# Two attention layers on one core: the last v tile of a batch computed behind the first mixing instead of ahead of the second step's scores

## The chip, the cores and the metric

The kernel runs on one core of a Trainium2 chip. TensorE (PE in the profile) multiplies matrices into PSUM, ScalarE (ACT) and VectorE (DVE) read PSUM and write SBUF, GpSimd (POOL) does a few vector operations and issues some transfers, and SyncE (SP) issues most transfers. The metric is the device time of one execution in microseconds, as the median of several runs; smaller is better.

## The reference

The input is x of shape 8 x 512 x 32 x 32 in float32: eight batch elements (called batches here), 512 channels, 1024 positions. Two layers follow one another, each as x = x + layer(group_norm(x)).

Layer 0 is a plain attention block with 8 heads of 64 channels. Layer 1, in which the change lies, is attention whose scores are mixed between heads before the softmax:

```python
q = jnp.einsum('oc,bct->bot', w_q, xf).reshape(b, heads, hd, t)   # k, v likewise
attn = jnp.einsum('bhdq,bhdT->bhqT', q, k) * scale
attn = jnp.einsum('gh,bhqT->bgqT', w_head, attn)      # heads are mixed
attn = jax.nn.softmax(attn, axis=-1)
# the map of each head is then normalised by its mean and variance, with gamma and beta
out = jnp.einsum('bhqT,bhdT->bhqd', attn, v)
out = out @ w_proj.T + b_proj
```

All arithmetic is in float32.

## The kernel before

The first 1800 us are layer 0, batch by batch; the rest is layer 1, again batch by batch. All engines run their instructions in the order in which the program emits them (the whole is written under a manual schedule), so the order of calls in the source is the order of each queue.

**Layer 1, one batch.** Queries are cut into NT = 8 tiles of 128. A batch runs nine steps p = 0 to 8 of four quarters t = 0 to 3 (`Attention1.step`, L1847). Three kinds of work overlap, each one step behind the one before:

- `scores(p, i)`, L1621, i = 0 to 7: four matmuls into one two-bank PSUM buffer (L1628), then a copy to SBUF (`raw`), by ScalarE (L1640), and in step 0 for odd i by VectorE (L1638). Scores 0 to 3 fill one raw buffer, 4 to 7 a second one; there are two.
- `regroup(p, kh, s)`, L1642: when a raw buffer is full, SP issues two transfers for each of four slots, SBUF to SBUF, into the tile `re` (L1646), so that the heads of one query lie side by side. Sixteen transfers of 256 KB a step.
- `mix(p - 1, s)`, L1656, s = 0 to 3: matmuls with the head-mixing matrix, from `re` into two two-bank PSUM buffers (L1665), and two exponentials by ScalarE into a tile `e` (L1678).
- `flip(p - 1, s)` and `moments(p - 1, s)`, on VectorE: a transpose of `e` in 32 x 32 blocks into `et` (L1693), and four calls of batch statistics (L1704).
- `values(p - 2 or p - 1, u, ...)`: matmuls of v with `et` (L1720); they need the flips. Later `sums` (the `zz` rows, VectorE) and `totals` (z, L1757, TensorE) make the softmax sums.

In step 0 there are only scores. In step 1 scores of the second query tile come with the first mixings, and no values until its last quarter. From step 2 on all kinds overlap.

**v.** The v projection of a batch is eight tiles of 128 positions x 512 channels, each four matmuls of 128 x 128 weights (a tile of y) against 512 columns of the v weights. Each float32 matmul appears twice in the profile, so a tile is eight TensorE rows. `v_pair(b, i)` (L1446) computes two tiles into one two-bank PSUM buffer, then copies the first to SBUF on ScalarE (L1458) and the second on VectorE (L1459). Pairs 0 and 1 are made at the end of the batch before (for batch 0 by L1030), pairs 2 and 3 in step 0 of the batch's own attention.

**The place.** Work that belongs to no step is put into an `Agenda` under a slot number. `step` runs slot 4p + t at the end of each quarter, and some half slots inside a quarter: slot 4p - 0.5 in quarter 0, directly after `mix(p - 1, 0)` and ahead of `flip(p - 1, 0)`. Pair 2 stands in slot 1, pair 3 in slot 3, the end of step 0. In batch 0 `v_sums` (L1463, 128 small matmuls at L1471) follows in slot 3.

**Buffers.** `m_psum` (L1283) hands out three two-bank PSUM buffers in turn, to scores, mixings, v pairs and projections; a buffer is free again when its last reader is done. The y of a batch and its v are single buffers of the pool `shared` (L654): the load of the next batch's y, of which `piece` emits one quarter a step from step 1 on (L1337, on SP), waits until the last reader of the present y is done. The v weights lie in one of two buffers that `et` uses too.

Of the kernel before, what the change touches and what calls it, by code (L numbers as in the profile page):

```python
# [467 lines left out]
def tile_two_attention_layers(  # L468
# [19 lines left out]
    nc = tc.nc  # L488
# [175 lines left out]
    def group_stages(b0, b1, psum):  # L664

        gs = GroupStats(
            gstat, psum, mvs[:, b0:b1].rearrange("p b c s -> p (b c) s"), f"1_{b0}", keep=1
        )

        def end():  # L670
            gs.root()
            at = slice(b0 * NCC, b1 * NCC)
            nc.vector.tensor_copy(gmean[:, at], gs.gm)
            nc.vector.tensor_copy(grstd[:, at], gs.r1)
            nc.vector.scalar_tensor_tensor(
                gneg[:, at], gs.gm, -1.0, gs.r1, ALU.mult, ALU.mult
            )
            nc.vector.scalar_tensor_tensor(
                ys[:, b0:b1].rearrange("p b c -> p (b c)"), gs.dm, float(T), gs.r1,
                ALU.mult, ALU.mult,  # L680
            )

        return gs.means, gs.squares, end
# [13 lines left out]
    with ExitStack() as l0:  # L697
# [87 lines left out]
        n_t, xa_t, q_t, k_t, v_t = {}, {}, {}, {}, {}  # L785
# [89 lines left out]
        def combine_right(nm, n):  # L875

            if not tmp:
                for i in range(7):
                    tmp[i] = epool.tile([P, 2, FB], F32, tag="e", name=f"tmp_{nm}_{i}")
            b11, b12, b21, b22 = (n[:, 2 * i : 2 * i + 2, ts(j, FB)] for i in (0, 1) for j in (0, 1))  # L880
            nc.vector.tensor_sub(tmp[0], b12, b11)
            nc.vector.tensor_sub(tmp[1], b22, tmp[0])
            nc.vector.tensor_sub(tmp[2], b22, b12)
            nc.vector.tensor_sub(tmp[3], b21, tmp[1])
# [318 lines left out]
        for b in range(B):  # L1203
            more = b + 1 < B
            ag = Agenda()
# [61 lines left out]
    with ExitStack() as l1:  # L1267
# [15 lines left out]
        def m_psum(nm):  # L1283
            return ps_m.tile([P, 2, FB], F32, tag="m", name=nm)
# [4 lines left out]
        y_t, qo_t, k_t, v_t = ({0: t["1"]} for t in (n_t, q_t, k_t, v_t))  # L1289
# [12 lines left out]
        def left_piece(key, f, n):  # L1302

            if f == 0:
                left_tile(key)
            nc.sync.dma_start(
                out=w_t[key][:, f : f + n].rearrange("p f o -> p (f o)"),
                in_=left_d[key[0] + "1"][:, 2 * f * HC : 2 * (f + n) * HC],
            )
# [16 lines left out]
        def p_piece(c):  # L1326

            if c == 0:
                left_tile(("p", B - 1))
                w_t["p", B - 1] = w_t["p", B - 1][:, :NCC]  # L1330
            nc.sync.dma_start(out=w_t["p", B - 1][:, c], in_=w_projT[ts(c, P)])

        def y_piece(b, c):

            if c == 0:
                y_t[b] = shared.tile([P, NCC, T], F32, tag="n", name=f"y_{b}")
            nc.sync.dma_start(out=y_t[b][:, c], in_=x1_d[b][ts(c, P), :])  # L1337

        def normalize1(b, c):
            normalize_to(y_t[b][:, c], b, c)  # L1340
# [74 lines left out]
        def right_tile(b):  # L1415

            right_t[b] = rawpool.tile([P, 4, 2, FB], F32, tag="raw", name=f"right_{b}")

        def left_p(b):

            t = rawpool.tile([P, H * FB], F32, tag="raw", name=f"left_p_{b}")
            load_left(("p", b), t[:, : 14 * HC])

        def right_y(b, parts=range(4)):
            combine_right(right_t[b], y_t[b], parts)

        def k_projection(b):
            t = k_t[b] = shared.tile([P, NCC, T], F32, tag="k", name=f"k1_{b}")

            def finish(i, j, x, y):  # L1430
                dst = t[:, 2 * i : 2 * i + 2, ts(j, FB)]
                if y is None:
                    nc.scalar.copy(dst, x)
                else:
                    nc.vector.tensor_add(dst, x, y)

            return Projection(f"pk1_{b}", ("k", b), y_t[b], right_t[b], finish)
# [3 lines left out]
        def k_leave():  # L1441
            for fn in due:
                fn()
            due.clear()

        def v_pair(b, i):  # L1446

            if i == 0:
                v_t[b] = shared.tile([P, NT, C], F32, tag="v", name=f"v1_{b}")
            ps = m_psum(f"pv1_{b}_{i}")  # L1450
            w = w_t["v", b]
            for m in range(2):
                for c in range(NCC):
                    nc.tensor.matmul(  # L1454
                        ps[:, m], y_t[b][:, c, ts(2 * i + m, P)], w[:, c],
                        start=(c == 0), stop=(c == NCC - 1),
                    )
            nc.scalar.copy(v_t[b][:, 2 * i], ps[:, 0])  # L1458
            nc.vector.tensor_copy(v_t[b][:, 2 * i + 1], ps[:, 1])  # L1459

        vs = const_tile("vs", [P, H, B])

# [34 lines left out]
        def out_view(b):  # L1497


            return qo_t[b].rearrange("p (n two) a t -> p n (two a t)", two=2)  # L1500
# [413 lines left out]
        def load_wv(b):  # L1914

            t = etpool.tile([P, 8 * H * 64], F32, tag="et", name=f"wv_{b}")[:, : NCC * C]
            load_w(("v", b), wvT, t)
# [3 lines left out]
        NV = NT // 4  # L1921
        for b in range(B):
            more = b + 1 < B
            a = Attention1(b)
            ag = Agenda()
            for i in range(NV):
                ag.at(1 + 2 * i, lambda i=i: v_pair(b, NV + i))
            if b == 0:
                stages = group_stages(B - 1, B, small_psum1)
                for i in range(3):  # L1930
                    ag.at(i, stages[i])
                ag.at(3, v_sums)
            if more:
                a.pieces += [lambda c=c: y_piece(b + 1, c) for c in range(NCC)]
                a.pieces += [lambda f=f: left_piece(("k", b + 1), f, 2) for f in (0, 4)]
                ag.at(4 * NT, lambda: left_piece(("k", b + 1), 2, 2))
                ag.at(4 * NT, lambda: left_piece(("k", b + 1), 6, 1))
                for c in range(NCC):
                    ag.at(20 + c, lambda c=c: normalize1(b + 1, c))

                def k_go(*ms):
                    if not kp:
                        kp.append(k_projection(b + 1))
                    for m in ms:
                        kp[0].products(m)
                        due.append(lambda m=m: kp[0].leave(m))

                kp = []
                ag.at(4 * NT - 0.5, lambda: right_tile(b + 1))
                ag.at(4 * NT - 0.5, lambda: k_go(1))  # L1950
                ag.at(4 * NT, lambda: right_y(b + 1, [0, 1]))
                ag.at(4 * NT + 0.5, lambda: k_go(2))
                ag.at(4 * NT + 1, lambda: right_y(b + 1, [2, 3]))
                ag.at(4 * NT + 1, lambda: left_p(b))
                ag.at(4 * NT + 1.5, lambda: k_go(6))
                ag.at(4 * NT + 2.5, lambda: k_go(7))
            else:
                a.pieces += [lambda c=c: p_piece(c) for c in range(NCC)]
            for p in range(NT + 1):
                for t in range(4):  # L1960
                    a.step(p, t, ag)
            ag.flush()
            k_leave()
            last = NT - 1
            a.sums(last)
            if not more:
                a.values(last, 0, 2, 3)
                a.leave(last, 0)
                a.values(last, 1, 0, 1, 2, 3)
                a.leave(last, 1)  # L1970
                a.totals(last)
                a.instance()
                out1_last(a)
                continue
            k_go(5)
            a.values(last, 0, 2, 3)
            a.leave(last, 0)
            load_wv(b + 1)
            a.values(last, 1, 0, 1, 2, 3)
            a.leave(last, 1)  # L1980
            a.totals(last)
            a.instance()
            k_leave()
            k_go(4, 3)
            k_leave()
            a.instance_end()
            v_pair(b + 1, 0)
            a.divide(NCH - 1)
            for g in range(H):
                a.affine(g)  # L1990
            right_o = re_t[:, 4:8]
            combine_right(right_o, out_view(b))
            op = out1(b, right_o)
            load_left(("q", b + 1))
            v_pair(b + 1, 1)
            a.check()
            op.run()
            q_projection(b + 1).run()
# [70 lines left out]
```

## Time and profile before

| what | value |
|---|---|
| median of 3 runs | 3999.17 us (3997.65 to 4006.88) |
| the profiled execution's own time | 3999.31 us |
| its span, first to last instruction | 3997.5 us |
| layer 1 within it | from about 1800 us to the end |
| TensorE busy | 3885.5 us (97%) |
| VectorE busy | 2834.6 us (71%) |
| ScalarE busy | 1971.3 us (49%) |
| mean granted TensorE clock | 0.995 |
| v tile rows L1454 | 480, in 30 calls of `v_pair` (16 rows each) |
| last v pair of batch 3 | 2653.20 to 2660.33 us |
| batch 3's first score of step 1, first mixing, first flip, first z | 2660.26, 2663.00, 2666.68, 2686.12 us |

Rows of the timeline give start, length, engine, line, operation, output <- inputs, shapes, the number of merged rows, and in brackets how long the engine had been idle and who released it. A merged TensorE row can hold short waits inside itself, so its length can exceed its work. The list of waits gives the total, the number of times and the longest. In a chain of waits each line is what released the next one. A DMA row of a queue is the issue of the transfer; when it lands is read from the updates of its semaphore in the trace.

### The profile page before, as it was taken

Reading aid. Unit: us, or ns where it says so; the run is one execution under the profiler, and the core shown is the slowest. Engines: PE = TensorE matmul, PEld = TensorE weight load, DVE = VectorE, ACT = ScalarE, POOL = GpSimd, SP = SyncE. Lnnn points to the kernel's source line nnn. Section 1 sums busy time; section 2 is a strip of 40 time slices with the busy share of each in tenths; the row PEclk is TensorE's granted clock in tenths of the full one; section 3 lists DMA queues with packets and bytes.
Section 4 is the critical chain, followed back from the end, with each engine's and each line's share of the span. In section 5 each row is a group of like instructions: output and inputs, shape, how many; then the busy total and the mean of one; then the engine's idle time right before and its main releaser. Section 6 shows DMA issues by size and latency. Waiting matters only on the chain.

```text
span 3997.5 us, 95841 instructions
## 1 busy us (share of the span) xinstructions
PE 3885.5 (97%) x41932; PEld 1826.1 (46%) x41932; DVE 2834.6 (71%) x4124; ACT 1971.3 (49%) x2431; POOL 128.5 (3%) x150
## 2 busy tenths in 40 slices
PE   8999999999999999999999999999999999999997
PEld 4353535344343535344544535545545445445354
DVE  4748475766657584857958949859769679588597
ACT  1726363544536271615717528437257166175274
POOL 0000000000000000000100000000001000000010
PEclk9999999999999999999999999999999999999999
DMA  3313131111121111217828749658469288397384
GB/s 121 120 48 117 46 120 48 62 59 66 53 83 54 72 68 61 75 66 184 230 92 226 190 120 237 173 137 227 148 164 228 99 210 207 97 232 198 107 219 127
DMA packets 245883, 519.10 MB, mean 130 GB/s; under 512 B 47312, under 2 KB 54480, under 8 KB 238800
## 3 DMA queue, kind: packets, MB, share of 16 engines
q1 hardware_dynamic: 238912, 497.95, 43.2%
q0 software_dynamic: 6544, 14.94, 1.7%
q8 instruction: 331, 5.42, 0.6%
q14 instruction: 96, 0.79, 0.1%
HBM read 197.16 MB, written 46.92 MB: 61 GB/s over the span
## 4 chain that ended last, share of the span: by engine, by line
PE 81%; DVE 13%; ACT 2%; DMA 2%; issue 2%; SPq 0%; DVEq 0%
PE s L1084 11%; PE a L1110 11%; PE a L1720 7%; PE s L1628 7%; DVE bn L1704 6%; PE pk_p L902 6%; PE pq_p L902 5%; PE pv L1454 5%; PE pv_p L902 5%; DVE et L1693 5%; PE pp_p L902 5%; PE pk L1379 4%; PE pq L1379 4%; PE pp L1379 4%; PE m L1665 4%
## 5 line engine op out<-in xcount | busy, mean ns | idle before, releaser
L1693 DVE STREAM_TRANSPOSE et<-e 128x2048 f32<-128x2048 f32 x256 | 587.3, 2294 | 88.7 <-ACT e L1678 86.8
L1720 PEld LDWEIGHTS a<-et,v 128*64 128x64 f32 x16384 | 509.2, 138 | 296.2 <-issue 247.6
L1704 DVE BATCH_NORM_STATS2 bn<-e 128x6 f32<-128x512 f32 x1024 | 634.3, 675 | 0.0
L1089 ACT ACTIVATE e<-s 128x1024 f32<-128x1024 f32 x512 | 497.2, 1026 | 234.5 <-PE s L1084 232.1
L1640 ACT COPY raw<-s 128x1024 f32<-128x1024 f32 x480 | 470.2, 1018 | 226.1 <-PE s L1628 197.5
L1720 PE MATMUL a<-et,v 128*64 128x64 f32 x16384 | 557.0, 225 | 12.1 <-DVE et L1693 11.4
L1678 ACT ACTIVATE e<-m 128x1024 f32<-128x1024 f32 x512 | 496.2, 1021 | 126.5 <-PE m L1665 54.2
L1097 DVE TENSOR_TENSOR zacc<-zacc,e 128x1024 f32<-128x1024 f32 x384 | 468.7, 1221 | 87.2 <-ACT e L1089 64.9
L1628 PE MATMUL s<-k,q 64*64 64x512 f32 x4096 | 516.0, 608 | 6.2 <-DVE q L1493 3.1
L1084 PE MATMUL s<-q,k 64*64 64x512 f32 x4096 | 490.1, 593 | 2.3 <-ACT e L1089 2.3
L1110 PE MATMUL a<-e,v 64*64 64x512 f32 x4096 | 484.1, 589 | 0.0
L1665 PE MATMUL m<-re,wmix 32*32 32x512 f32 x8192 | 315.3, 604 | 19.3 <-DMA re<-raw 17.8
L1110 PEld LDWEIGHTS a<-e,v 64*64 64x64 f32 x4096 | 156.7, 133 | 282.8 <-issue 282.2
L1084 PEld LDWEIGHTS s<-q,k 64*64 64x64 f32 x4096 | 147.9, 133 | 275.2 <-issue 240.7
L1628 PEld LDWEIGHTS s<-k,q 64*64 64x64 f32 x4096 | 127.7, 132 | 220.8 <-issue 78.2
L1454 PE MATMUL pv<-wv,y 128*128 128x512 f32 x480 | 212.1, 597 | 0.0
L1736 ACT COPY q<-a 64x256 f32<-64x256 f32 x256 | 93.7, 366 | 184.7 <-PE a L1720 182.7
L1772 POOL DMA_DIRECT2D zd<-rz x56 | 34.7, 619 | 3449.0 <-DVE r L1784 3449.0
L1454 PEld LDWEIGHTS pv<-wv,y 128*128 128x128 f32 x480 | 89.3, 190 | 116.9 <-issue 110.3
L1665 PEld LDWEIGHTS m<-re,wmix 32*32 32x32 f32 x8192 | 66.7, 103 | 148.9 <-ACT raw L1640 58.6
L1458 ACT COPY v<-pv 128x512 f32<-128x512 f32 x30 | 17.6, 585 | 218.7 <-PE pv L1454 218.7
L1095 DVE TENSOR_TENSOR zacc<-e,e 128x1024 f32<-128x1024 f32 x64 | 78.3, 1223 | 56.1 <-ACT e L1089 56.1
(315 smaller groups left out, 3942.4 us busy)
## 6 DMA issues: line engine op xcount, KB each, us to landing
re<-raw SPq DMA_DIRECT2D x1024, 256.0 KB
left_q<-left_q SPq DMA_DIRECT2D x17, 1792.0 KB
left_p<-left_p SPq DMA_DIRECT2D x17, 1792.0 KB
left_k<-left_k SPq DMA_DIRECT2D x10, 1792.0 KB
x<-in_x_dram SPq DMA_DIRECT2D x32, 512.0 KB
rzb<-zd SPq DMA_DIRECT2D x128, 128.0 KB
x<-x SPq DMA_DIRECT2D x64, 256.0 KB
y<-x SPq DMA_DIRECT2D x32, 512.0 KB
```

The lines of the kernel that those rows point to most:

```text
L902: nc.tensor.matmul(out, st, mv, start=start, stop=(k == 1), skip_group_check=True)
L1084: nc.tensor.matmul(ps[c * D : c * D + D, m], k[r, hp, k0 : k0 + D], q[r, hp, ts(f, FB)], start=True, stop=True,)
L1089: nc.scalar.activation(e[i], ps, AF.Exp, scale=S0 * S0)
L1110: nc.tensor.matmul(acc[g][a][m * D : m * D + D], v[rows, kc, ts(2 * hp + m, D)], e[i][rows, m], start=(kc == 0), stop=(kc == NG - 1),)
L1379: nc.tensor.matmul(self.ps[m][:, i], w[:, left, k * HC + i * P : k * HC + i * P + P], right[:, k], start=(k == 0 and m != 2), stop=(k == 1 ...
L1454: nc.tensor.matmul(ps[:, m], y_t[b][:, c, ts(2 * i + m, P)], w[:, c], start=(c == 0), stop=(c == NCC - 1),)
L1628: nc.tensor.matmul(ps[c * D : c * D + D, m], qo_t[b][r, p, hp, ts(c, D)], k_t[b][r, hp, ts(kh, FB)], start=True, stop=True,)
L1665: nc.tensor.matmul(ps[a // 2][c * 32 : c * 32 + 32, a % 2].rearrange("p (r h k) -> p h r k", r=2, h=2), wmix[rows].rearrange("p g i -> p ( ...
L1678: nc.scalar.activation(e[:, :, 2 * h : 2 * h + 2].rearrange("p r a k -> p a r k"), ps[h].rearrange("p a (r k) -> p a r k", r=2), AF.Exp,)
L1693: nc.vector.transpose(self.et[p, u].rearrange("p kb (r st a) g q -> p st kb r (a g q)", r=2, st=2)[:, st], self.e[p, s].rearrange("p r a ( ...
L1704: nc.vector.bn_stats(self.bn[p][:, s, a], e[:, :, a].rearrange("p r k -> p k r"))
L1720: nc.tensor.matmul(acc[two * D : two * D + D, s].rearrange("p (x q) -> p x q", q=4), v_t[b][:, kb, ts(g, D)], et[:, kb, :, g], start=(kb = ...
```

## The change

`v_pair` takes a list of tiles, `ms`, of the pair to compute; called without it, it does both as before. Each call requests its own PSUM buffer. Pair 3 of every batch is split. Its first tile (with its ScalarE copy) stays in slot 3, at the end of step 0. Its second tile (with its VectorE copy) goes to slot 3.5, which `step` runs in quarter 0 of step 1: behind scores 0, 1, 2 and the first mixing, ahead of the first flip. Pair 2 stays in slot 1. In batch 0 `v_sums` now lies between the two tiles.

```diff
-        def v_pair(b, i):
+        def v_pair(b, i, ms=range(2)):
 
             if i == 0:
                 v_t[b] = shared.tile([P, NT, C], F32, tag="v", name=f"v1_{b}")
-            ps = m_psum(f"pv1_{b}_{i}")
+            ps = m_psum(f"pv1_{b}_{i}_{ms[0]}")
             w = w_t["v", b]
-            for m in range(2):
+            for m in ms:
                 for c in range(NCC):
                     nc.tensor.matmul(
                         ps[:, m], y_t[b][:, c, ts(2 * i + m, P)], w[:, c],
                         start=(c == 0), stop=(c == NCC - 1),
                     )
-            nc.scalar.copy(v_t[b][:, 2 * i], ps[:, 0])
-            nc.vector.tensor_copy(v_t[b][:, 2 * i + 1], ps[:, 1])
+            for m in ms:
+                copy = nc.vector.tensor_copy if m else nc.scalar.copy
+                copy(v_t[b][:, 2 * i + m], ps[:, m])
...
-            for i in range(NV):
-                ag.at(1 + 2 * i, lambda i=i: v_pair(b, NV + i))
+            ag.at(1, lambda: v_pair(b, NV))
+            ag.at(3, lambda: v_pair(b, NV + 1, [0]))
+            ag.at(3.5, lambda: v_pair(b, NV + 1, [1]))
```

## The prediction

> **What bounds the kernel now.** I read the page first, then the waits of TensorE, then the chain of waits around the place that changes, then the rows of the engines there. I use batch 3 of layer 1 throughout; batches 1, 2 and 4 to 7 have the same row lengths there within 0.02 us, and batch 0 differs by one extra block (L1471). The page, part 1:
>
> ```profile
> PE 3885.5 (97%) x41932; PEld 1826.1 (46%) x41932; DVE 2834.6 (71%) x4124; ACT 1971.3 (49%) x2431; POOL 128.5 (3%) x150
> ```
>
> 97% suggests no slack on TensorE, yet moving work pays only where TensorE really stands. The list of TensorE's waits:
>
> ```profile
> PE z L1757 <- DVE zz L1750: 29.1, 27, 2.1
> PE m L1665 <- DMA re<-raw: 17.8, 11, 3.3
> PE a L1720 <- DVE et L1693: 11.4, 10, 5.3
> PE m L1665 <- ACT e L1678: 1.4, 8, 0.2
> ```
>
> The z and a waits are for VectorE. Their first ones in each batch lie just behind the place that changes. The chain of waits in batch 3 (start, length, what):
>
> ```profile
> 2653.27 7.06 PE pv L1454 x16
> 2660.33 2.74 PE s L1628 x24
> 2663.07 1.61 PE m L1665 x29
> 2664.68 0.02 issue
> 2664.71 1.95 ACT e L1678 x2
> 2666.65 0.02 issue
> 2666.68 2.31 DVE et L1693
> 2668.99 1.01 DVE bn L1704 x2
> ...
> 2685.76 0.23 DVE zz L1750
> 2685.98 0.14 issue
> 2686.12 0.39 PE z L1757 x4
> ```
>
> So the path is: v pair, three scores and the first mixing on TensorE; the exponentials on ScalarE; then VectorE without a pause from 2666.68 to 2685.98 (four flips and moments, then zz); then TensorE again at z. While VectorE carries the path, TensorE stalls, as its timeline shows (start, length, instruction, idle before):
>
> ```profile
> 2663.00 1.58 PE L1665 MATMUL m<-re,wmix 32*32 32x512 f32 x32
> 2664.51 1.09 PE L1628 MATMUL s<-k,q 64*64 64x512 f32 x8
> 2665.78 2.05 PE L1665 MATMUL m<-re,wmix 32*32 32x512 f32 x32 [0.18 <-ACT e L1678]
> 2670.05 1.94 PE L1665 MATMUL m<-re,wmix 32*32 32x512 f32 x32
> 2673.64 1.15 PE L1720 MATMUL a<-et,v 128*64 128x64 f32 x32 [0.63 <-DVE et L1693]
> 2675.75 1.16 PE L1665 MATMUL m<-re,wmix 32*32 32x512 f32 x32
> ```
>
> A mixing takes 1.16 us when nothing holds it (2675.75) and 1.58, 2.05 and 1.94 in the first three quarters, where it waits in mid-group for PSUM to be emptied. From 2660.26 to 2673.64, 13.38 us, TensorE has six scores (0.91 each, from 2.74 for three) and three mixings (about 1.08 net of overlap): 5.5 + 3.2 = 8.7 us of work, so 4.7 us of hole, more than one v tile.
>
> [...] 97%, and a third of those 13.38 us is hole. [...] The three two-bank buffers here do rotate, and the 2.05 us mixing is that rotation running out. [...] every engine's rows follow the order in the code. This decides the prediction: the moved tile's copy stands in VectorE's queue ahead of the first flip. [...] Here a regrouping transfer's row is 0.53 us, and its semaphores finish 3.2 us after its start (2654.63 to 2657.83).
>
> **The change, part by part.** Times below are us after the first score of the second step (2660.26 before), called tau.
>
> *Removed at the end of step one.* Four fp32 matmuls, recorded as eight. A v pair of sixteen takes 7.06 us from its first row to the next group's; a second pair directly behind one costs 6.87 (14.00 - 7.13, the 32-record blocks). Half of 6.87 is 3.43 us. Its eight weight loads (0.19 us each) overlap and cost nothing apart. The first score of step two then starts 3.43 us earlier, if nothing else holds it. Its PSUM buffer was emptied earlier (the copies of scores 6 and 7 end by 2654.6), and the regrouping transfers that free its raw buffer landed by 2655.3. The other tile's ScalarE copy (0.58 us) stays where it is and is over before the first raw copy, as before. VectorE's copy (0.69 us) leaves; VectorE idles there (6.43 us before it), so that is worth 0.
>
> *Does the first mixing find its data?* It needs the tenth regrouping transfer of step one, at 2658.95 by the DMA semaphores. The mixing starts at 2663.00 now and would at 2659.57: the margin falls from 4.05 us (4.04 to 4.08 in batches 1 to 7, 7.88 in batch 0) to 0.62, of which about 0.14 is the wake-up seen where this wait does bind (the last mixing row of steps, e.g. 2812.45 to 2812.59). Hidden, by 0.5 us. The transfers themselves do not move: they are issued after the copy of score 7, ahead of the tile.
>
> *Added: the tile behind the first mixing.* Its PSUM buffer is the one of the third score, emptied at tau 4.05; the mixing ends at 4.25. So it starts at 4.2 and TensorE is free at about 7.9 (3.43 + 0.2 for the change of group, as 7.07 against 6.84 = 16 x 0.4275 shows). A pair's first copy starts 7.17 us after its first matmul; eight records less, 3.74. So VectorE's copy runs from about 7.97 to 8.6. The first flip, ready at 6.42 as before (exponentials don't depend on the tile), stands behind it and starts at about 8.6. That is the wait that the change adds: **2.2 us on the VectorE chain** (bounds 2.1 and 2.3: next row 0.61 or 0.69 us after the copy's start). Behind the flip stand all moments, flips and zz of this step, and behind these TensorE's a and z.
>
> *Everything else in the hole.* The fourth score (7.9), its raw copy (9.0 to 10.0), the second mixing (8.8; its second buffer is the tile's, empty at 8.6) and its exponentials (10.1 to 12.1) are late by 2 us too, but the second flip needs them only at 8.6 + 4.62 = 13.2. Third exponentials end at 16.3; third flip at 17.8. Values wait for the second flip until 15.5, as they do now until 13.38. From there all engines stand to one another as now. Cost 0; without VectorE's chain as cover these scores would cost the tile's full 3.4 us.
>
> *Queues.* SP: the load of the next batch's y (512 KB, L1337) writes the single y buffer that the tile still reads, so its issue moves from 2661.25 to the tile's end, about 2664.8. Behind it on SP stand step two's regroupings, due when score 3's raw copy ends (now 2667.57, then about 2666.9): 1.5 us to spare after its 0.6 us issue. Those regroupings come 0.6 us later against the flips than now. The next mixing that needs the group's tenth transfer has 0.53 to 1.43 us of margin, and TensorE's 1.23 us wait at z follows, so up to about that much is absorbed: 0. POOL issues nothing here. The weights wv keep their et buffer longer, until the third flip asks for it at 17.8: 0. The extra PSUM request shifts the rotation by one: 0.
>
> *Sum.* Per batch -3.43 + 2.2 = -1.23 us; eight batches have one such place (in batch 0 with v_sums between, and 3.4 us at half clock): **-9.8 us**. The profiled execution took 3999.31 us (span 3997.5, so 1.8 around it), which gives 3989.5; the median of the runs, 3999.17, lies 0.14 from it, so the forecast is 3989.4 either way: 0.25% less.
>
> **Rivals.**
> *Whole gain* (VectorE's delay is swallowed, or the copy comes before the exponentials end): 8 x 3.43 = 27.4 us, 3971.8. For: VectorE is only 71% busy. Against: it has no pause at all from the first flip to z, and TensorE waits there in every batch. Part of it, 12 to 20 us, if the copy comes earlier than worked out or a wait later in the batch shortens.
> *Nothing gained*: the tile delays the chain by its full length, e.g. because the mixing's release or the y load's place pushes the regroupings by more than z absorbs: 3999.2.
> *Slower*: the first mixing comes to wait for the regrouping. It decides from a tenth landing 0.5 us later than now; the gain is used up at 0.5 + 1.23 = 1.7 us later, and 0.3% is lost from 3.3 us later. For: later in each batch the same kind of wait does bind, 1.2 to 3.3 us. Against: at this place seven batches agree within 0.04 us, and the transfers' start does not move. At 3.5 us later: +1.8 x 8 = 14 us, 4013.
>
> **How the numbers follow.** A measurement of this kernel can tell about 0.3% (12 us) from no change. The forecast's own case 0.58 (3986.5 to 3991.5; one time in twelve or so a measurement of it crosses 12 us), more than 12 us gained 0.22, nothing gained 0.11, slower 0.09. Hence faster 0.27, same 0.64, slower 0.09. The range 3978 to 4000 holds the first case, the nearer half of the second and nearly all of the third.
>
> **What would show it.** Right: in each batch eight pv records ahead of the scores and eight behind the first mixing; the time from first score to that mixing still 2.74; a VectorE v copy directly ahead of the first flip, and that flip 2.2 us later after the first score (8.6 against 6.42); values at 15.5 against 13.38; z still waiting about 1.2 us; TensorE's mixings 1.1 to 1.2 rather than 2 us. Wrong: a wait for re<-raw at the first mixing, a first flip that starts at the exponentials' end, or a z wait that vanishes.

## The result, and the profile after

Over 22 runs of each kernel, taken turn by turn, the changed kernel has a median of 3996.7 us (3986.82 to 4004.14) and the kernel before 4001.79 us (3994.13 to 4010.3). The ratio is 0.9983, with a 95% interval of 0.9976 to 0.9989: 6.8 us or 0.17% faster (4.4 to 9.6 us). Two later sets of runs of the same changed kernel gave 0.9979 (0.9968 to 0.9990) and 0.9983 (0.9975 to 0.9992). That lies inside the predicted range and on the side that was forecast; the size forecast, 0.25% (9.8 us), was too large by 3 us. The prediction took 0.3% as the least that a measurement can tell from no change; with 22 runs of each kernel the interval is 0.13% wide and excludes no change. The profiled execution took 3989.87 us with a span of 3988.1, which is 9.4 us less than the first span before.

In the profiles below the lines of the code behind `v_pair` have moved by one: L1665 of before is L1666, and so on. The list of TensorE's waits after the change (total, times, longest):

```profile
PE z L1758 <- DVE zz L1751: 27.8, 26, 2.1
PE m L1666 <- DMA re<-raw: 20.5, 13, 3.4
PE a L1721 <- DVE et L1694: 6.9, 9, 4.5
```

The wait of the values for the flip (a, for et) has fallen by 4.5 us, and the wait of the mixing for the exponentials (m, for e) is gone from the list. The wait for the regrouping has grown from 17.8 to 20.5 us (18.4 and 19.7 in a second trace of each kernel). The chain of waits at the same place of batch 3:

```profile
2660.28 2.74 PE s L1629 x24
2663.01 1.51 PE m L1666 x29
2664.53 3.65 PE pv L1454 x8
2668.17 0.02 issue
2668.20 0.69 DVE v L1460
2668.89 2.22 DVE et L1694
...
2688.22 0.39 PE z L1758 x4
```

Before, the path went from the mixing over the exponentials to the first flip. Now it goes from the mixing through the moved tile and its VectorE copy to the first flip; the exponentials are ready 2 us earlier and wait. TensorE's timeline:

```profile
2662.94 1.58 PE L1666 MATMUL m<-re,wmix 32*32 32x512 f32 x32
2664.46 3.70 PE L1454 MATMUL pv<-wv,y 128*128 128x512 f32 x8
2669.11 1.16 PE L1666 MATMUL m<-re,wmix 32*32 32x512 f32 x32
2672.50 1.94 PE L1666 MATMUL m<-re,wmix 32*32 32x512 f32 x32
2675.76 1.15 PE L1721 MATMUL a<-et,v 128*64 128x64 f32 x32 [0.30 <-DVE et L1694]
```

The second mixing takes 1.16 us where it took 2.05: its buffers are free by the time it starts. The third still takes 1.94.

The table gives the starts of the first mixing, the first flip, the first values and z, in us after the first score of step 1. Batch 0, with its extra block (L1471), is left out.

| | first mixing | first flip | values | z |
|---|---|---|---|---|
| before, batches 1 to 7 | 2.74 | 6.41 | 13.38 | 25.85 |
| predicted | 2.74 | 8.6 | 15.5 | 28.0 |
| after, batches 1 and 3 to 7 | 2.74 | 8.59 | 15.55 | 28.02 |
| after, batch 2 | 3.87 | 9.30 | 16.27 | 28.72 |

### The profile page after: what moved, and what is told of

The parts are those of the page before. It is cut to its first block, busy times and chain, and to the rows that moved or that the text cites. A ratio compares the mean times of both kernels' runs of the same rounds, so it can differ in the third digit from the quotient of the medians.

```text
span 3988.1 us, 95834 instructions
## 1 busy us (share of the span) xinstructions
PE 3881.3 (97%) x41932; PEld 1825.2 (46%) x41932; DVE 2832.9 (71%) x4124; ACT 1974.8 (50%) x2431; POOL 128.7 (3%) x150
## 4 chain that ended last, share of the span: by engine, by line
PE 81%; DVE 13%; issue 2%; DMA 2%; ACT 2%; SPq 0%; DVEq 0%
PE s L1084 11%; PE a L1110 11%; PE a L1721 7%; PE s L1629 7%; DVE bn L1705 6%; PE pk_p L902 6%; PE pq_p L902 5%; PE pv L1454 5%; DVE et L1694 5%; PE pv_p L902 5%; PE pp_p L902 5%; PE pk L1379 4%; PE pq L1379 4%; PE pp L1379 4%; PE m L1666 4%
## 5 line engine op out<-in xcount | busy, mean ns | idle before, releaser
L1694 DVE STREAM_TRANSPOSE et<-e 128x2048 f32<-128x2048 f32 x256 | 587.6, 2295 | 47.7 <-ACT e L1679 44.7
L1666 PE MATMUL m<-re,wmix 32*32 32x512 f32 x8192 | 308.8, 608 | 21.1 <-DMA re<-raw 20.5
L1460 DVE COPY v<-pv 128x512 f32<-128x512 f32 x30 | 20.7, 690 | 160.4 <-PE pv L1454 81.7
L1666 PEld LDWEIGHTS m<-re,wmix 32*32 32x32 f32 x8192 | 65.5, 103 | 142.4 <-ACT raw L1641 59.8
```

Source lines behind the costliest of these rows:

```text
L1666: nc.tensor.matmul(ps[a // 2][c * 32 : c * 32 + 32, a % 2].rearrange("p (r h k) -> p h r k", r=2, h=2), wmix[rows].rearrange("p g i -> p ( ...
L1694: nc.vector.transpose(self.et[p, u].rearrange("p kb (r st a) g q -> p st kb r (a g q)", r=2, st=2)[:, st], self.e[p, s].rearrange("p r a ( ...
```

## The experiments

My theory was that of the prediction: removing the tile ahead of the scores wins 3.43 us a batch, and its copy, standing ahead of the first flip in VectorE's queue, gives 2.2 us of it back, one to one. The rivals were that VectorE does not set the end and only TensorE's hole counts, that the first mixing comes to wait for the regrouping, and, for the part of the gain that was missing, the granted clock. Every kernel was timed beside the kernel before.

**The copy on ScalarE.** Only the engine of the moved tile's copy changes.

```diff
             for m in ms:
-                copy = nc.vector.tensor_copy if m else nc.scalar.copy
+                copy = nc.vector.tensor_copy if m and len(ms) > 1 else nc.scalar.copy
```

> The changed kernel, but the moved v tile is copied out of PSUM by ScalarE, so that nothing stands ahead of the first flip in VectorE's queue. Theory of the prediction (the copy ahead of the flip costs the VectorE chain 2.2 us a batch): the first flip starts at 6.4 us after the first score of the second step again (8.6 in the changed kernel); the chain is then held only at its second flip, which waits for the exponentials of the second mixing at about 12.1 (11.0 before), so values and z are 1.1 us later than before and not 2.2; gain 3.43 - 1.1 = 2.3 us a batch, 17 to 19 us against before (about 0.45%). Rival (the VectorE chain isn't what sets the end, the gain is the idle time of TensorE that is filled): the same time as the changed kernel, 7 to 10 us below before.

Measured: 3984.37 us, ratio 0.9947 (0.9932 to 0.9962), 21 us below before (15 to 27). VectorE's rows in batch 3, whose first score is at 2658.28:

```profile
2664.69 2.31 DVE L1694 STREAM_TRANSPOSE et<-e 128x2048 f32<-128x2048 f32 x1 [8.68 <-ACT e L1679]
2666.92 2.48 DVE L1705 BATCH_NORM_STATS2 bn<-e 128x6 f32<-128x512 f32 x4
2670.44 2.31 DVE L1694 STREAM_TRANSPOSE et<-e 128x2048 f32<-128x2048 f32 x1 [1.04 <-ACT e L1679]
```

The first flip starts at 6.41 again, at the end of the exponentials, and the second one waits 1.04 us for its own. z stands at 27.00, 1.15 us later than before, as expected:

```profile
2685.27 0.39 PE L1758 MATMUL z<-sel,zz 128*64 128x32 f32 x4
```

Moving one copy of 0.6 us to another queue about tripled the gain. This is what the theory says and the rival excludes: TensorE's work and order are those of the changed kernel. Two things did not follow the expectation. The values come at 15.18, 1.8 us later than before and not 1.1, because now TensorE itself reaches them late (it does not wait there); its wait at z, 1.2 us before, shrinks to 0.6 us or less and hides this. And z is only 1.0 us earlier than in the changed kernel, which is 8 us in eight batches, of the 14 measured between the two. The mean clock of these five runs, 0.9944 against 0.9937 in the first 22 runs of the changed kernel, accounts for some 3 us more at the rate found below; the rest is within the interval.

**A delay on VectorE alone.** In the kernel before, the first flip of each batch is done twice; no other work moves (dst and src stand for the two views of L1694 and L1695).

```diff
-                nc.vector.transpose(dst, src)
+                for _ in range(2 if (p, s) == (0, 0) else 1):
+                    nc.vector.transpose(dst, src)
```

> The kernel before, with the first flip of each batch done twice on VectorE (same output). It measures by itself what a VectorE delay at this place is worth. Theory: it passes one to one: values and z 2.2 us later in every batch, 17 to 19 us slower than before (0.45%). Rival (VectorE, 71% busy, has slack that swallows it): 0.

Measured: 4023.12 us, ratio 1.0050 (1.0035 to 1.0064), 20 us slower (14 to 26). Values stand at 15.72 (+2.34) and z at 28.3 (+2.5) in batches 1 to 7. So a delay here passes to the end. But TensorE's rows show more than a delay:

```profile
2687.97 1.15 PE L1721 MATMUL a<-et,v 128*64 128x64 f32 x32 [2.98 <-DVE et L1694]
2689.06 1.81 PE L1628 MATMUL s<-k,q 64*64 64x512 f32 x8
2690.80 2.01 PE L1665 MATMUL m<-re,wmix 32*32 32x512 f32 x32
```

Behind the stall of 2.98 us a score takes 1.81 us and a mixing 2.01, where they take 1.09 and 1.16: the granted clock is at half for 3.4 us. The 1.23 us that TensorE otherwise waits at z hid most of that.

**Half of that delay.** Ahead of the first flip, half of it is done once more.

```diff
+                if (p, s) == (0, 0):
+                    nc.vector.transpose(dst[:, 0:4], src[:, 0:4])
                 nc.vector.transpose(dst, src)
```

> The kernel before, with half of the first flip of each batch done once more ahead of it on VectorE (same output): half the delay of double_flip, 1.15 us. In all traces so far a TensorE stall of 2 us or more is mostly followed by 3.4 us at half clock, one of under 1.5 us hardly ever; the stall at the values, 0.63 us before, grows to 2.9 in double_flip and to 1.8 here. Theory (VectorE delay passes one to one, the half clock comes on top and only behind long stalls): 8 to 11 us slower than before, z 1.2 us later, mean clock within 0.001 of before. Rival (the half clock follows the delay whatever its length): 15 us or more slower, mean clock 0.992 or less.

Measured: 4014.18 us, ratio 1.0030 (1.0020 to 1.0040), 12 us slower (8 to 16); z at 27.13 in five of the eight batches, +1.27. The delay passes one to one (1.27 x 8 = 10 us). The mean clock of the timed runs was 0.9928, against 0.9944 for before beside them: 0.0016 lower, more than the 0.001 that I allowed and less than the rival's. The stall at the values was 1.91 us, and in three of the eight batches TensorE ran at half clock behind it, with no wait left at z. Batch 3 is one of them:

```profile
2691.76 1.15 PE L1721 MATMUL a<-et,v 128*64 128x64 f32 x32 [1.91 <-DVE et L1697]
2692.85 1.98 PE L1628 MATMUL s<-k,q 64*64 64x512 f32 x8
```

So half clock sets in behind stalls of just under 2 us too, only less often (the counts are in the last section).

**Both tiles behind the first mixing.**

```diff
-            ag.at(3, lambda: v_pair(b, NV + 1, [0]))
-            ag.at(3.5, lambda: v_pair(b, NV + 1, [1]))
+            ag.at(3.5, lambda: v_pair(b, NV + 1))
```

> Both tiles of the last pair behind the first mixing. Theory: the first mixing, which would start 6.9 us earlier than before, now meets the landing of the tenth regrouping transfer and waits about 2.9 us for it (it starts 3.9 us earlier than before); the pair of 7.1 us and its copies then hold the first flip until 1.9 us later than before: about 15 us slower than before (0.4%). Rival (regrouping lands earlier when the mixing asks earlier, or does not bind): mixing 6.9 us earlier, first flip 1 us earlier than before, 8 us faster than before. Rival without a VectorE chain: 4 us a batch faster, 30 us.

Measured: 4029.96 us, ratio 1.0062 (1.0047 to 1.0077), 25 us slower (19 to 31). TensorE in batch 3:

```profile
2677.70 1.15 PE L1666 MATMUL m<-re,wmix 32*32 32x512 f32 x32 [3.30 <-DMA re<-raw]
2678.78 8.83 PE L1454 MATMUL pv<-wv,y 128*128 128x512 f32 x16
```

The first mixing starts at 6.0 after the first score instead of 2.74, 0.14 us behind the landing of the tenth regrouping transfer, in seven batches of eight. So the limit that the prediction saw is there and lies where it said: asking earlier does not make the transfers land earlier (the tenth lands 4.33 to 4.40 us after the ninth's issue in these batches, 4.29 to 4.33 before). The sign is right, the 15 us were too few: the pair behind the stall of 3.3 us takes 8.83 us instead of 7.13, again at half clock (a mean of 0.72 from 2677.5 to 2681.0). In each of the seven batches the mixing and the pair together lose about 1.7 us in this way. Seven times 1.7 us is 12 us, and 15 + 12 = 27 lies within the interval.

**The tile one quarter later.**

```diff
-            ag.at(3.5, lambda: v_pair(b, NV + 1, [1]))
+            ag.at(4.5, lambda: v_pair(b, NV + 1, [1]))
```

> The changed kernel with the moved tile one quarter later, behind the second mixing and ahead of the second flip; its copy still on VectorE. Theory: first flip at 6.4 us after the first score as before; the copy at 11.3 to 11.9 holds the second flip by about 0.9 us (11.9 against 11.0), and the third exponentials, late behind the tile, end just when the third flip is due; so 3.43 - 0.9 = 2.5 us a batch gained, 17 to 20 us against before. Rival (only filling TensorE's hole counts): as the changed kernel, 7 to 10 us.

Measured: 3997.89 us, ratio 0.9991 (0.9984 to 0.9999), 4 us faster (0.4 to 6). A miss: the first flip is at 6.41 and the second at 11.85, as expected, yet z comes at 26.9 to 29.2 instead of 26.8. SP's rows (first fence) and TensorE's (second) in batch 3, whose first score is at 2661.39:

```profile
2672.62 0.34 SPq L1337 DMA_DIRECT2D y<-x  x1
2673.06 13.60 SPq L1647 DMA_DIRECT2D re<-raw  x16
```

```profile
2688.08 1.27 PE L1666 MATMUL m<-re,wmix 32*32 32x512 f32 x32 [2.11 <-DMA re<-raw]
```

The load of the next y waits on SP for the moved tile, which still reads the single y buffer. The regroupings of step 1 stand behind it on the queue: they could start when the fourth score is copied, at 7.3, and start at 11.7. The mixing of step 2 then waits for them, 0.55 to 2.11 us in seven of the eight batches. The prediction worked this queue out for the change itself, where 1.5 us were to spare; the expectation of this experiment left it out.

**The same with the load out of the way.** Pieces of the next batch's loads begin in step 2 instead of step 1.

```diff
-                if old and t == 0:
+                if older and t == 0:
                     self.piece()
```

> The tile behind the second mixing, as in slot45, and the first quarter of the next batch's y loaded one step later (pieces from step 2 on). Theory from the trace of slot45: there the y load waits on SP for the moved tile, the regroupings of step 1 stand behind it (first issue 11.7 us after the first score, 7.3 were possible) and behind its 512 KB, and the mixing of step 2 waits 0.6 to 2.1 us a batch for them. Without that the mixing doesn't wait, z stands 26.9 us after the first score (28.4 in slot45, 25.9 before): 2.4 us a batch gained, 17 to 21 us below before. Rival (the tile between second mixing and fourth score delays TensorE's own later work by that much, whatever the loads do): as slot45, 2 to 6 us below before.

Measured: 3986.66 us, ratio 0.9955 (0.9942 to 0.9969), 18 us faster (12 to 23). z stands at 26.91, and the mixing of step 2 waits 0.16 us in one batch and not at all in the others. So it was the y load, not the place of the tile. Whether its place on the queue or its 512 KB held the regroupings more was not separated, though their late start (11.7 instead of 7.3) is the queue's alone.

**More room for the first mixing.** The copy is on ScalarE as above, and the single tile and the pair of step 0 change places.

```diff
-            ag.at(1, lambda: v_pair(b, NV))
-            ag.at(3, lambda: v_pair(b, NV + 1, [0]))
+            ag.at(1, lambda: v_pair(b, NV + 1, [0]))
+            ag.at(3, lambda: v_pair(b, NV))
```

> The moved tile copied by ScalarE, as in act_copy, and the single tile and the pair of step 0 exchanged, so that the pair lies between the last score of step 0 and the first mixing. The first mixing's margin over the regrouping goes from 0.6 to about 2 us; all else as in act_copy. Theory that late regroupings at the first mixing cost the change part of its gain: 1 to 3 us better than act_copy, 20 to 24 us below before. Rival (these waits are rare and short): the same as act_copy within its interval.

Measured: 3982.95 us, ratio 0.9947 (0.9934 to 0.9961), 21 us faster: the ratio of the copy on ScalarE. The margin did go from 0.6 to 1.4 us or more in every batch, and no first mixing waits, so the waits there are too rare to be seen in the time. The rival stands. Both kernels beat the changed one by about 14 us.

**The two kernels once more.**

> The kernel before, once more, for the spread of its times, its granted clock and the waits of a second trace: 0 against before; places of step 1 within 0.05 us of the first trace, waits for regrouping 16 to 21 us in all, 7 to 10 stretches of 3.4 us at half clock in layer 1.

> The changed kernel, once more, for a second trace. The gain was worked out as 9.8 us and measured as 6.8. Theory that late regroupings at the first mixing take the rest: the first mixing waits in one to three of eight batches, 1 us each, 2 to 3 us in all. Rival (the granted clock is at half more often): no such waits, but ten or more stretches of 3.4 us at half clock in layer 1 against eight before, 1.7 us each. 5 to 10 us below before.

> The changed kernel, once more, for the granted clock of its timed runs beside those of before on the same chip. Theory (3 us of the gain that was worked out are lost to more time at half clock): mean clock 0.0005 to 0.001 below that of before, time 5 to 9 us below before. Rival (the clock is the same on average, the difference was chance): clocks equal within 0.0003, and 9 to 11 us below before.

Measured: the kernel before against itself 0.9996 (0.9987 to 1.0004), with 18.4 us of waits for the regrouping and eight stretches at half clock in layer 1, as expected; the changed kernel 3996.85 and 3997.98 us, with the ratios given above. The places of step 1 repeat to 0.05 us in all traces of a kernel, batches 0 and 2 apart. The first mixing of the changed kernel waits for the regrouping in one batch of eight, the same one, batch 2, in each of its three traces. In the first:

```profile
2385.23 1.15 PE L1666 MATMUL m<-re,wmix 32*32 32x512 f32 x32 [1.06 <-DMA re<-raw]
```

In the other two it waits about 0.4 and 0.2 us. So these waits took 1 us at most; the theory of 2 to 3 us falls. What is left is the clock. In the last set its mean was 0.9933 in the changed kernel against 0.9944 in the kernel before, 0.001 lower, as the theory said and its rival (equal clocks) did not. Put together, 99 timed runs of before have a mean time of 4003.3 us at a mean granted clock of 0.9945, and 55 of the changed kernel 3996.3 us at 0.9936. Among runs of one kernel the time rises by about 4 us for each 0.001 of clock that is lost (a line through the 99 runs gives 4.1, through the 55 runs 3.9). Runs with the same clock compare as follows; the few at other clocks are left out.

| clock of the run | before: runs, mean us | changed: runs, mean us | difference |
|---|---|---|---|
| 0.993 | 10, 4008.9 | 24, 3999.4 | 9.5 |
| 0.994 | 38, 4005.5 | 18, 3994.3 | 11.2 |
| 0.995 | 31, 4001.8 | 6, 3989.5 | 12.3 |
| 0.996 | 16, 3996.4 | 2, 3988.6 | 7.8 |

At equal clock the change is worth some 10 us (one line for each kernel with a common slope gives 10.7, with a 95% interval of 0.9 on either side); 0.0009 of clock takes 3 to 4 of them back.

## Why the prediction was right

**What is removed, 3.43 us a batch:** right. The single tile takes 3.63 us from its first row to the next group's in the chain of waits (2656.64 to 2660.28 in batch 3), and a pair took 7.06.

**The first mixing finds its data:** right in seven batches. The margin is 0.59 to 0.62 us in batches 1 and 3 to 7 (0.62 forecast). In batch 2 it is used up (the last section says by what). The rival that this wait eats the gain had a place and a limit, and moving the pair showed both, but for one tile it costs 1 us in all.

**The wait that the change adds, 2.2 us on VectorE:** right, 8.59 - 6.41 = 2.18 us. That it passes to the end was shown from both sides, by taking the copy out of the queue (z 1.0 us earlier) and by adding a delay of that size to the kernel before (z 2.5 us later).

**Everything else in the hole, cost 0:** right for the path; z still waits 0.95 to 1.24 us for VectorE. Two details were wrong and cost nothing. The third mixing was to take 1.1 to 1.2 us and still takes 1.94: in its middle it waits until 13.0 for ScalarE's copy of a score that holds its second buffer, 0.8 us after its start, and the working didn't follow that buffer. And TensorE has seven scores, not six, in the 13.38 us before the values (the row at 2671.93 in batch 3 is the seventh), so at the prediction's own 0.91 us a score the hole was 3.8 us rather than 4.7, still more than the tile's 3.43.

**SP's queue:** right for the change. The y load is issued at 2668.19, the end of the tile, and the regroupings at 2670.28, 2.1 us behind it (1.5 to spare behind the issue of 0.6 were forecast). The same queue made the version one quarter later nearly worthless.

**The sum, 9.8 us:** measured 6.8. The part that the working can see is confirmed by 10 us at equal clock. The term that was missing is the granted clock: the working took it as unchanged, apart from one stretch in batch 0, and gave no reason. The 0.0009 of clock are about two more stretches of 3.4 us at half clock in a run (an estimate: 0.0009 x 4000 us, divided by the 1.7 us that half of 3.4 us makes). With one of 6.8 us counted as two, the traces show 10, 11 and 15 of them in the changed kernel and 8 and 10 in the kernel before, from 1800 us on and without the last stretch at the kernel's end. TensorE stalls of 2 us or more number 8, 10 and 12 against 8 and 8, counted from 1900 us to 3960 us. Most of them are the waits of the last step for the regrouping and of z for VectorE, which last from 1 to over 3 us in both kernels, and they are not at the place of the change. Whether such a stall leads to half clock does not follow from its length alone, as the last section shows (2.40 us without it, 2.34 us with it), so five traces are too few to say why the changed kernel has more; that stays open, although the clock of the timed runs shows that it is no accident of these traces.

**The whole-gain rival** (27 us) fell: the copy's own delay is real. What was right in it is that the delay is avoidable, and the copy on ScalarE gets 21 us.

## What to carry to other kernels

When work is moved into a hole of one engine, follow its evacuation too: here the copy's place ahead of the flip in VectorE's queue cost two thirds of what the matmuls gained (2.2 of 3.43 us), and ScalarE, which copied the pair's other tile out of PSUM in 0.59 us, was idle at that moment (for 2.65 us in batch 3). Look at what the moved work still reads: a load that reuses that buffer waits longer, and what stands behind it on its queue waits with it (with the tile one quarter later, the regroupings started at 11.7 us instead of 7.3). And where the clock falls after a stall, as here after 83 of the 109 stalls of over 2 us, a stall costs more than its length (up to 1.7 us more for each 3.4 us at half clock), so count the stalls of that kind, and not only the total of idle time.

## What the runs showed of the hardware

Behind some stalls TensorE's granted clock stood at half for 3.4 us, now and then for 6.8. In the first profile of the changed kernel, the wait for the regrouping in the last step of batch 1 takes 2.41 us and ends at 2257.29, and the clock is at 0.50 from 2257.20 to 2260.61. Between 1900 and 3900 us, the twelve traces of this study hold 98 such stretches, and every one starts between 1 us before and 3.5 us after the end of a TensorE stall of over 0.4 us. Longer stalls were followed by half clock more often: 83 of the 109 of over 2.0 us, 13 of the 52 between 1.5 and 2.0 us, and 12 of the 336 shorter ones.

Length is not all. Two executions of the kernel before show this at the same wait for the regrouping, in the last step of batch 1. The columns are the stretch, its length, the busy time of PE, PEld, DVE, ACT and POOL with instruction counts, the granted clock, and the DMA's share and GB/s. In the first execution the stall takes 2.40 us and ends at 2258.78, and the clock stays at 1.00:

```profile
2257.40:2260.81 3.41, 2.03 (x34) 0.76 (x35) 3.41 (x5) 0.69 (x1) 0.00 (x0) 1.00 1.00 253
```

In the second one it takes 2.34 us, and behind it the clock is at 0.50:

```profile
2259.43:2262.84 3.41, 3.41 (x35) 1.09 (x4) 3.15 (x8) 1.94 (x2) 0.00 (x0) 0.50 1.05 248
```

What decides between the two was not shown.

Each 3.4 us at half clock cost up to 1.7 us of TensorE time (8.83 us for a pair that otherwise takes 7.13, with both tiles behind the first mixing), unless a later wait hid it, as with the doubled flip. That the time of a run rises by 4 us for each 0.001 of clock fits a loss in full: 0.001 of 4000 us is 4 us. Single runs of the kernel before have mean clocks from 0.991 to 0.997 and times from 4020 down to 3991 us, which is more than the change itself is worth. Why the clock differs so much from run to run was not shown; the timed runs have no traces.

A transfer of the regrouping landed 3.2 us after its issue when its queue was free (the ninth of step 0, 2654.63 to 2657.83 in batch 3 of the kernel before) and about 1.07 us behind the one before it when it was not. That asking for it earlier changes nothing was expected; that batch 2 is late by up to 1 us in every trace of the changed kernel was not. There, the ninth transfer's sixteen semaphore updates come as in the other batches, the fifteenth 3.1 us after the issue, except for the last one, which comes 0.8 to 1.7 us behind it. In each of these traces a packet of the DMA queue q8, which the page calls "instruction", starts 1.0 to 1.8 us after that issue. In the two traces of the kernel before it starts within 0.1 us of the issue, and the landing is not late. In batches 1 and 3 to 7 of the changed kernel no packet of q8 starts within 5 us after the issue, and the transfer is never late. That this packet delays the transfer fits all of these; no experiment moved it.
